# Two images loaded in six parts over three cycles; mixed weights in three slots; the centre's copy one slot later

## The chip, the cores and the metric

The kernel runs on one core of a Trainium2 chip. A core has a matrix engine (PE, with its own queue PEld for loading weights), a vector engine (DVE), a scalar engine (ACT), GpSimd (POOL), and a queue engine (SP). Each works through its own instructions in the order in which they were written, and waits for the others by semaphores alone. DMAs are issued here by SP and by POOL; all of them share sixteen DMA engines. The metric is the device time of one execution in microseconds (us), the median of several runs.

## The reference

The input is four images of 128 channels by 96 x 96 pixels, float32. Two layers follow each other, and each is a non-local block (attention of every pixel to pooled pixels of its own image):

```
g     = maxpool2(conv1x1(x, g_w, g_b))        # 64 channels, 2304 values
phi   = maxpool2(conv1x1(x, phi_w, phi_b))    # 64 channels, 2304 keys
theta = conv1x1(x, theta_w, theta_b)          # 64 channels, 9216 queries
y     = softmax(theta^T phi) g                # over the 2304 keys
out   = batchnorm(conv1x1(y, W_w, W_b)) + x
```

Per image and layer that is a 9216 x 2304 matrix of scores, its exponentials, and their product with the values. The four images are independent; the second layer of an image needs the whole of its first.

## The kernel before

**Blocks, pairs, steps, cycles.** Image and layer make a block; there are eight, in the order `ORDER`: (0,0), (1,0), (0,1), (2,0), (1,1), (3,0), (2,1), (3,1). In this text image 1 to 4 are indices 0 to 3. A block's queries go in nine *pairs* of 2 x 512, and a pair goes through the 18 key tiles in nine *steps* of two tiles, so the whole program is one loop (variable `t`) over 648 steps. Two pairs are a *cycle* of 18 steps (`CYCLE`); a step's place in its cycle is called `s`. Cycle 0 is steps 0 to 17, cycle 2 is steps 36 to 53.

**One step.** PE makes the scores of two key tiles (line 591, sixteen 64x64 matmuls), ACT takes exponentials (line 596) into one of six buffers, DVE adds them up for the denominators (line 605), and PE multiplies the exponentials of the step before by the values (line 613). Between these stands all the rest, at fixed places written out by hand. Dictionaries give the step at which something is issued: `after` (weights), `tails` (filled by `later`), `stages` (matmuls of the units, below), `loads` (images). Everything in `after` and `tails` is issued at the end of its step. No scheduler moves it.

**Ends of a pair.** Every pair's denominators are turned, inverted by DVE (`invert`, at s = 13 for the even pair, at s = 6 of the next cycle for the odd one), written by SP to a row (line 685, `stage<-both`) and spread by SP over 64 partitions in four DMAs (line 689, `halves<-stage`; here "the broadcast"). `normalise` multiplies by it at s = 1 and s = 10, and PE projects at s = 3 and s = 13 (line 705). POOL adds the result to the image in place by an accumulating DMA (line 720, `x<-halves`).

**Units: the next block's keys.** While one block is computed, the keys and values of the next are made in six *units* of 16 image rows, two per cycle in three cycles. For each, SP copies pieces of the image (lines 422 to 427: `load`, `load_rest`), POOL adds others to them by accumulating DMAs (line 419: `add_one`, `add_two`, and a last one), at s = 10, 11, 12, 12, 15 for the first unit of a cycle and at s = 0, 1, 2, 2, 4 of the next cycle for the second (`BUILDS`). PE uses the sums in four stages (`UNITS`: s = 15, 16, 0, 2 and s = 7, 8, 10, 12). The second stage (line 448) is the first that needs `add_two`. DVE then pools (line 502); for a block's first unit it also computes the keys' mean (`centring`, lines 513 and 514, one step after the fourth stage), and ACT copies that mean to the other 64 partitions (line 517). One step later `spread` writes the centred keys (ACT, lines 532 and 536). Two PSUM banks (`two_banks`) serve the units' stages, the thetas and the projections in turn.

**Weights.** `steps_mixed` makes differences and sums of the layer's g and phi weights that the units multiply by. It returns two steps: `crossed`, three ACT copies across partitions (lines 197 to 199), and `combined`, five DVE operations (lines 202 to 206) and a fourth ACT copy (line 207) that reads the result of line 204. For the first layer both stand at the end of step 9. For the second layer the list `steps` holds 13 entries (4 for g and phi, 2 mixed, 2 theta, 5 for W), three per cycle at s = 2, 7 and 11 from cycle 1 on: `crossed` at step 43, `combined` at step 47, theta at 56 and 61, W at 65, 74, 79, 83 and 92.

**Images.** Three image buffers exist. Image 1 and image 2 are loaded at the start. The others are loaded whole, six DMAs of 768 KB in a row on SP, before step 43 (image 3) and step 285 (image 4):

```
    loads = {4 * NB + 7: 2, 31 * NB + 6: 3}
...
            if t in loads:
                xs[loads[t]] = load_x(loads[t])
```

Image 4 takes the buffer of image 1, whose last store is issued at step 258. The first units that read image 3 are built from step 172 on, those of image 4 from step 334 on.

Of the kernel before, what the change touches and what calls it, by code (L numbers as in the profile page):

```python
# [9 lines left out]
F32 = mybir.dt.float32  # L10
# [7 lines left out]
B, C, CI, H, W = 4, 128, 64, 96, 96  # L18
HW = H * W
# [16 lines left out]
NB = NKT // KB  # L36
FIRST = 6
UR = 16
NU = H // UR
# [16 lines left out]
CYCLE = 2 * NB  # L56
# [6 lines left out]
def shifted_blocks(ctx: ExitStack, tc: tile.TileContext, x: bass.AP, layers, out: bass.AP, flag):  # L63
# [24 lines left out]
    nc = tc.nc  # L88
# [3 lines left out]
    xp = ctx.enter_context(tc.tile_pool(name="xp", bufs=3))  # L92
# [24 lines left out]
    for i, limit in enumerate((SUM_MAX, 1.0 / SUM_MIN)):  # L117
        nc.vector.memset(limits[:, i : i + 1], limit)

    def load_x(b, n=6):  # L120
        xt = xp.tile([C, HW], F32, tag="x", name=f"x_{b}")
        src = x[b].rearrange("c h w -> c (h w)")
        for i in range(n):
            nc.sync.dma_start(out=xt[:, ts(i, HW // n)], in_=src[:, ts(i, HW // n)])  # L124
        return xt

    def as_row(src):
# [20 lines left out]
    class Layer:  # L148
# [40 lines left out]
        def steps_mixed(self):  # L189

            low, high = slice(0, CI), slice(CI, P)
            g, phi = slice(0, CI), slice(CI, 2 * CI)
            m = self.mixed = const.tile([P, 3, CI], F32, name=f"mixed_{self.l}")
            w = self.gphi

            def crossed():
                nc.scalar.copy(m[low, 1, :], w[high, phi])
                nc.scalar.copy(m[high, 2, :], w[low, g])
                nc.scalar.copy(m[high, 1, :], w[low, phi])

            def combined():
                nc.vector.tensor_sub(m[low, 0, :], w[low, phi], m[low, 1, :])
                nc.vector.tensor_sub(m[high, 0, :], m[high, 1, :], w[high, phi])
                nc.vector.tensor_sub(m[high, 0, :], m[high, 0, :], m[high, 2, :])
                nc.vector.tensor_sub(m[high, 1, :], m[high, 2, :], m[high, 1, :])
                nc.vector.tensor_add(m[high, 2, :], w[high, g], m[high, 0, :])
                nc.scalar.copy(m[low, 2, :], m[high, 0, :])

            return [crossed, combined]

        def steps_theta(self):
            self.theta = const.tile([C, CI], F32, name=f"thetaT_{self.l}")
# [60 lines left out]
    class Block:  # L273
# [94 lines left out]
        def centring(self, n):  # L368

            centre, gphi = self.centre, self.gphi
            nc.vector.tensor_reduce(centre[CI:, :], gphi[CI:, : n * KT], AX.X, ALU.add)
            nc.vector.tensor_scalar(
                centre[CI:, :], centre[CI:, :], -1.0 / (n * KT), None, ALU.mult
            )
# [6 lines left out]
        def copied(self, keys):  # L383

            nc.scalar.copy(self.phi[:CI, keys], self.phi[CI:, keys])
# [14 lines left out]
    class Unit:  # L400
# [65 lines left out]
        def second(self):  # L466
            self.part(self.blk.w.mixed[CI:, 0, :], sums[1][CI:, :, : UN // 2], 0)
# [43 lines left out]
        def centring(self):  # L511
            centre = self.blk.centre
            nc.vector.tensor_reduce(centre[:CI, :], self.keys[:CI, 2 * UK :], AX.X, ALU.add)
            nc.vector.tensor_scalar(
                centre[:CI, :], centre[:CI, :], -1.0 / (2 * UK), None, ALU.mult
            )
            nc.scalar.copy(centre[CI:, :], centre[:CI, :])

        def parts(self):

# [6 lines left out]
        def spread(self):  # L527
            src = self.keys[:, 2 * UK :].rearrange("p (b k) -> p b k", k=32)
            planes = self.blk.planes().rearrange("p i (t k) -> p i t k", k=KT)
            for m, n, k, t in self.parts():  # L530
                dst = planes[:, :, t : t + n, ts(k, 32)]
                nc.scalar.activation(
                    dst[:, 0], src[:, m : m + n, :], AF.Identity, bias=self.blk.centre
                )
                for h in range(2):
                    nc.scalar.copy(dst[ts(1 - h, CI), 1], dst[ts(h, CI), 0])
# [233 lines left out]
    def thetas(both):  # L770
# [15 lines left out]
    ws = [Layer(l, p) for l, p in enumerate(layers)]  # L786
    ws[0].load_gphi((nc.scalar, nc.sync))
    xs = {0: load_x(0, 12)}
    ws[0].load_theta(nc.scalar)
    first_cols = columns(  # L790
# [4 lines left out]
    other_cols = columns(  # L795
        [(w, key) for w in ws for key in rest] + [(ws[1], "theta_b")], "other", nc.sync
    )
# [49 lines left out]
    for k in range(KT // 32):  # L847
        b0.square(0, k)
    xs[1] = load_x(1)


    after = {8: [other_cols], 9: ws[0].steps_mixed()}
    for i, step in enumerate(ws[0].steps_W()):
        after[10 + i] = [step]
    after[9] += [lambda: ws[1].load_gphi((nc.sync, nc.sync)), lambda: ws[1].load_theta(nc.sync)]
    after[16] = [lambda: ws[1].load_W(nc.sync)]
    steps = [lambda i=i: late_steps("gphi", i) for i in range(4)]
    steps += [lambda i=i: late_steps("mixed", i) for i in range(2)]
    steps += [lambda i=i: late_steps("theta", i) for i in range(2)]
    steps += [lambda i=i: late_steps("W", i) for i in range(5)]  # L860
    made = {}
# [1 line left out]
    def late_steps(what, i):  # L863
        if i == 0:
            made[what] = getattr(ws[1], f"steps_{what}")()
        made[what][i]()
# [8 lines left out]
    def later(t, step):  # L875
        tails.setdefault(t, []).append(step)

    for n in range(1, len(blocks)):
        cycle = (n - 1) * NP * NB // CYCLE * CYCLE
        for u in range(NU):  # L880
# [14 lines left out]
            later(when[2], unit.spread)  # L895
            for i in range(2):
                later(when[3 + i], lambda unit=unit, i=i: unit.square(i))
    loads = {4 * NB + 7: 2, 31 * NB + 6: 3}
    late = len(pairs) - 2

    ends = {
# [4 lines left out]
    for t in range(total + 1):  # L906
        q, s = 2 * (t // CYCLE), t % CYCLE
        even, odd = pairs[q : q + 2] if t < total else (None, None)
        first, second, take = None, *pending
        pending = (None, None)  # L910
        unit, stage_of = stages.get(t, (None, None))
        assert unit is None or (t not in keys and second is None)
        if t in keys:
            n, i = keys[t]
            first, *pending = blocks[n].chunks(i)
        elif unit:
            first = (unit.first, unit.second, unit.third, unit.fourth)[stage_of]
            second = unit.second_rest if stage_of == 1 else None
            take = (unit.first_sum, unit.second_sum, unit.third_sum, unit.fourth_sum)[stage_of]
        elif t < total and s == THETAS[q > 0]:  # L920
            if q < late:
                first, *pending = thetas(pairs[q + 1 : q + 3])
            else:
                first, take = odd.theta_alone()
        elif t == total - 1:
            second, take = even.multiply, even.add
        elif gone and s in PROJECT:
            pair = gone[PROJECT.index(s)]
            second, take = pair.multiply, pair.add
            later(t + STORE, pair.put)  # L930
        if t < total:
            now, j = divmod(t, NB)
            if s == 0 and q:
                gone = pairs[q - 2 : q]
            if t in loads:
                xs[loads[t]] = load_x(loads[t])
        for i in range(KB):
            if t < total:
                pairs[now].scores(j * KB + i, rowwise=stage_of == 1 and i == 1)
            if i == 0 and first:  # L940
                first()
        if second:
            second()
        for i in range(KB):
            if t < total:
                pairs[now].add_up(j * KB + i)
            if i == (stage_of == 1) and take:
                take()
        if t == 0:
            b0.batch(FIRST - 1)  # L950
        if t - 1 in keys and t < NB:
            b0.batch(keys[t - 1][1])
        if t:
            before, j = divmod(t - 1, NB)
            for k in ends.get(t, range(j * KB, (j + 1) * KB)):
                pairs[before].values(k)
        if t < total:
            for i, pair in enumerate(gone):
                if s == NORM[i]:
                    pair.normalise()  # L960
            for i, pair in enumerate((even, gone[1] if gone else None)):
                if pair is None:
                    continue
                if s in (TURNS[i], TURNS[i] + 1):
                    pair.turn(s - TURNS[i])
                sooner = q == late and i == 0
                if s == (TURNS[0] + 2 if sooner else HALVES[i]):
                    pair.add_halves()
                if s == (TURNS[0] + 2 if sooner else INVERT[i]):
                    pair.invert()  # L970
            if q == late and s == 15:
                even.normalise()
        if t == total - 1:
            odd.last_denominators()
        for i, k in squares.get(t, []):
            b0.square(i, k)
        for step in tails.pop(t, []):
            step()
        for step in after.pop(t, []):
            step()  # L980
# [323 lines left out]
```

## Time and profile before

| | |
|---|---|
| three runs | 2499.68, 2500.20, 2502.04 us (median 2500.2) |
| the profiled execution | 2500.54 us, of which its span is 2498.8 us |
| PE busy | 2474.1 us, 99% of the span |
| DVE, ACT, POOL busy | 88%, 67%, 10% |
| mean granted clock of PE | 0.997 of full |
| PE's longest wait | 13.4 us, once |

The span runs from the first to the last instruction; the remaining 1.74 us lie around it. "Busy" is the sum of an engine's instructions. A chain of waits leads back from an instruction to what released it. A line of a timeline gives start, duration, engine, kernel line, operation, written and read tiles, a count, and in brackets the idle time before and what ended it. A line of a window gives the window's length, then busy time and instructions (in brackets) of PE, PEld, DVE, ACT and POOL, the granted clock, the DMA engines' busy share, and GB/s. All start times are from the span's start.

A step is taken to begin with the first of its sixteen score matmuls in the timeline. In undisturbed cycles (all from cycle 20 on, for one) equal places take equal times to the hundredth: a cycle with two units takes 69.75 us, one without 65.23 us.

### The profile page before, as it was taken

Reading aid. Unit: us, or ns where it says so; the run is one execution under the profiler, and the core shown is the slowest. Engines: PE = TensorE matmul, PEld = TensorE weight load, DVE = VectorE, ACT = ScalarE, POOL = GpSimd, SP = SyncE. Lnnn points to the kernel's source line nnn. Section 1 sums busy time; section 2 is a strip of 40 time slices with the busy share of each in tenths; the row PEclk is TensorE's granted clock in tenths of the full one; section 3 lists DMA queues with packets and bytes.
Section 4 is the critical chain, followed back from the end, with each engine's and each line's share of the span. In section 5 each row is a group of like instructions: output and inputs, shape, how many; then the busy total and the mean of one; then the engine's idle time right before and its main releaser. Section 6 shows DMA issues by size and latency. Waiting matters only on the chain.

```text
span 2498.8 us, 56189 instructions
## 1 busy us (share of the span) xinstructions
PE 2474.1 (99%) x23391; PEld 931.2 (37%) x23391; DVE 2192.2 (88%) x2947; ACT 1671.2 (67%) x1836; POOL 254.6 (10%) x286
## 2 busy tenths in 40 slices
PE   9997999999999999999999999999999999999998
PEld 5354354333333333333333333333333333333333
DVE  7897988998889998999878998899987899877788
ACT  5665666666666676766666766676766676666665
POOL 0010111110011101110001110111100111000000
PEclk9998999999999999999999999999999999999999
DMA  6366445552366645657335673665434666333334
GB/s 185 44 83 122 52 54 70 70 71 25 26 83 95 89 52 67 93 73 132 27 27 80 99 100 35 95 80 71 53 21 45 80 81 97 43 44 43 43 36 61
DMA packets 101038, 171.72 MB, mean 69 GB/s; under 512 B 16030, under 2 KB 78120, under 8 KB 100776
## 3 DMA queue, kind: packets, MB, share of 16 engines
q1 hardware_dynamic: 65664, 94.11, 30.7%
q0 software_dynamic: 34944, 73.88, 19.5%
q8 instruction: 185, 3.03, 0.5%
q14 instruction: 77, 0.63, 0.1%
q10 hardware_dynamic: 168, 0.07, 0.0%
HBM read 19.21 MB, written 18.87 MB: 15 GB/s over the span
## 4 chain that ended last, share of the span: by engine, by line
PE 93%; DVE 3%; DMA 2%; ACT 1%; SPq 1%; issue 1%; POOL 0%; DVEq 0%; POOLq 0%; ACTq 0%
PE sc L591 42%; PE av L613 42%; PE unit_ps L442 3%; PE theta_ps L269 2%; PE W_ps L705 2%; DVE sum L605 1%; DMA halves<-stage 1%; DMA sums<-x 1%; PE unit_ps L448 1%; DMA sums<-sums 1%; PE gphi_ps L321 0%; ACT exp L596 0%; SPq L124 0%; SPq L689 0%; PE gphi_ps L269 0%
## 5 line engine op out<-in xcount | busy, mean ns | idle before, releaser
L596 ACT ACTIVATE exp<-sc,nshift 128x1024 f32<-128x1024 f32 x1296 | 1395.7, 1113 | 727.7 <-PE sc L591 703.2
L605 DVE TENSOR_TENSOR sum<-sum,exp 128x1024 f32<-128x1024 f32 x1151 | 1407.6, 1223 | 223.3 <-ACT exp L596 166.8
L591 PE MATMUL sc<-theta,phi 64*64 64x512 f32 x10368 | 1288.3, 590 | 3.0 <-ACT exp L596 2.9
L613 PE MATMUL av<-exp,gT 64*64 64x512 f32 x10368 | 1241.1, 589 | 0.0
L591 PEld LDWEIGHTS sc<-theta,phi 64*64 64x64 f32 x10368 | 415.8, 133 | 676.7 <-issue 612.9
L613 PEld LDWEIGHTS av<-exp,gT 64*64 64x64 f32 x10368 | 412.7, 133 | 684.4 <-issue 654.8
L419 POOL DMA_DIRECT2D sums<-x x84 | 81.3, 1140 | 1042.0 <-PE sc L591 543.5
L720 POOL DMA_DIRECT2D x<-halves x70 | 63.5, 907 | 1050.6 <-ACT halves L716 1028.1
L603 DVE TENSOR_TENSOR sum<-exp,exp 128x1024 f32<-128x1024 f32 x72 | 88.0, 1222 | 30.2 <-ACT exp L596 30.2
L664 DVE TENSOR_REDUCE parts<-turned 128x16 f32<-128x512 f32 x142 | 97.4, 686 | 4.9
L663 DVE STREAM_TRANSPOSE turned<-sum 128x512 f32<-128x512 f32 x142 | 100.1, 705 | 0.5
L419 POOL DMA_DIRECT2D sums<-sums x84 | 91.5, 1090 | 41.6 <-DMA sums<-sums 22.3
L620 ACT COPY halves<-av 128x1024 f32<-128x1024 f32 x71 | 72.0, 1014 | 35.4 <-PE av L613 35.4
L716 ACT ACTIVATE halves<-W_ps,shift 128x512 f32<-128x512 f32 x140 | 88.8, 693 | 0.7 <-PE W_ps L705 0.7
L502 DVE TENSOR_REDUCE stage<-stage 128x192 f32<-128x768 f32 x84 | 77.8, 941 | 0.0
L705 PE MATMUL W_ps<-halves,WT 64*64 64x512 f32 x568 | 75.2, 590 | 0.2 <-DVE stage L497 0.2
L543 DVE STREAM_TRANSPOSE gT<-stage 32x192 f32<-32x192 f32 (+1 forms) x224 | 71.5, 319 | 3.8
L269 PE MATMUL theta_ps<-x,thetaT 64*64 64x512 f32 x560 | 74.2, 589 | 0.0
L442 PE MATMUL unit_ps<-sums,mixed 64*64 64x384 f32 x504 | 69.3, 482 | 0.0
L676 DVE STREAM_TRANSPOSE four<-parts 32x32 f32<-32x32 f32 x284 | 56.4, 198 | 2.9
L699 DVE TENSOR_TENSOR halves<-halves 128x512 f32<-128x512 f32 x71 | 48.6, 685 | 7.9 <-DMA halves<-stage 7.8
L696 DVE TENSOR_TENSOR halves<-halves 128x512 f32<-128x512 f32 x71 | 48.5, 684 | 0.0
(113 smaller groups left out, 738.1 us busy)
## 6 DMA issues: line engine op xcount, KB each, us to landing
x<-halves POOLq DMA_DIRECT2D x70, 512.0 KB, 4.7
halves<-stage SPq DMA_DIRECT2D x284, 64.0 KB
out_dram<-x SPq DMA_DIRECT2D x35, 512.0 KB
sums<-x SPq DMA_DIRECT2D x42, 384.0 KB
sums<-x SPq DMA_DIRECT2D x84, 192.0 KB
sums<-x POOLq DMA_DIRECT2D x84, 192.0 KB, 4.6
sums<-sums POOLq DMA_DIRECT2D x84, 192.0 KB, 4.5
x<-in_x_dram SPq DMA_DIRECT2D x18, 768.0 KB
```

Source lines behind the costliest of these rows:

```text
L269: nc.tensor.matmul(out, lhsT=lhsT, rhs=rhs, start=step == 0, stop=step == 1)
L419: nc.gpsimd.dma_start(out=dst, in_=src, accum_op=ALU.add)
L442: nc.tensor.matmul(bank[ts(c, CI), :UN], lhsT=lhsT, rhs=rhs[:, c, :], start=True, stop=True)
L591: nc.tensor.matmul(ps[ts(c, CI), ts(h, QT)], lhsT=self.blk.keys_of(k, c, h), rhs=self.th[ts(h, CI), :], start=True, stop=True,)
L596: nc.scalar.activation(e, ps, AF.Exp, bias=nshift)
L603: nc.vector.tensor_add(self.sum, self.es[0], e)
L605: nc.vector.tensor_add(self.sum, self.sum, e)
L613: nc.tensor.matmul(self.av[ts(h, CI), ts(r, QT)], lhsT=self.blk.gT[ts(r, CI), k, :], rhs=e[ts(r, CI), ts(h, QT)], start=(k == 0), stop=(k ...
L663: nc.vector.transpose(self.turned, self.sum[:, ts(h, QT)])
L664: nc.vector.tensor_reduce(self.parts[:, ts(h, QT // SQ)], self.turned.rearrange("p (b k) -> p b k", k=SQ), AX.X, ALU.add,)
L705: nc.tensor.matmul(self.pss[h][ts(c, CI), :], lhsT=self.blk.w.W[ts(h, CI), ts(c, CI)], rhs=self.y[ts(h, CI), :], start=True, stop=True,)
L716: nc.scalar.activation(self.halves[:, ts(h, QT)], self.pss[h], AF.Identity, bias=self.blk.w.shift,)
```

## The change

Three things change.

1. Images 3 and 4 are loaded in the same six parts of 768 KB, but each part at a step of its own: image 3 at steps 43, 50, 61, 68, 79 and 86, image 4 at steps 266, 277, 284, 295, 302 and 313. All stand at s = 7 or s = 14, which is the step after one of the two `invert`s of a cycle, and so behind that one's broadcast on SP's queue.
2. `steps_mixed` returns three steps, the fourth ACT copy being the third (`copied`). For the first layer they stand at steps 7, 8 and 9. For the second layer the list grows to 14: `crossed` 43, `combined` 47, `copied` 56, theta 61 and 65, W at 74, 79, 83, 92 and 97 (so everything behind `combined` moves by one place).
3. The ACT copy of the mean (line 517) moves from `centring` to the start of `spread` of a block's first unit, one step later.

No work is added or taken away; the number of instructions on PE, DVE, ACT and POOL is the same, and so are all DMAs.

```diff
+    def new_x(b):
+        return xp.tile([C, HW], F32, tag="x", name=f"x_{b}")
+
+    def load_part(b, xt, i, n):
+        src = x[b].rearrange("c h w -> c (h w)")
+        nc.sync.dma_start(out=xt[:, ts(i, HW // n)], in_=src[:, ts(i, HW // n)])
+
     def load_x(b, n=6):
-        xt = xp.tile([C, HW], F32, tag="x", name=f"x_{b}")
-        src = x[b].rearrange("c h w -> c (h w)")
+        xt = new_x(b)
         for i in range(n):
-            nc.sync.dma_start(out=xt[:, ts(i, HW // n)], in_=src[:, ts(i, HW // n)])
+            load_part(b, xt, i, n)
         return xt
...
                 nc.vector.tensor_add(m[high, 2, :], w[high, g], m[high, 0, :])
+
+            def copied():
                 nc.scalar.copy(m[low, 2, :], m[high, 0, :])
 
-            return [crossed, combined]
+            return [crossed, combined, copied]
...
                 centre[:CI, :], centre[:CI, :], -1.0 / (2 * UK), None, ALU.mult
             )
-            nc.scalar.copy(centre[CI:, :], centre[:CI, :])
...
             planes = self.blk.planes().rearrange("p i (t k) -> p i t k", k=KT)
+            if self.u == 0:
+                nc.scalar.copy(self.blk.centre[CI:, :], self.blk.centre[:CI, :])
             for m, n, k, t in self.parts():
...
-    after = {8: [other_cols], 9: ws[0].steps_mixed()}
+    after = {8: [other_cols]}
+    for i, step in enumerate(ws[0].steps_mixed()):
+        after[7 + i] = after.get(7 + i, []) + [step]
...
-    steps += [lambda i=i: late_steps("mixed", i) for i in range(2)]
+    steps += [lambda i=i: late_steps("mixed", i) for i in range(3)]
...
-    loads = {4 * NB + 7: 2, 31 * NB + 6: 3}
+    loads = {
+        2 * CYCLE + 7 + i // 2 * CYCLE + i % 2 * 7: (2, i) for i in range(NU)
+    } | {
+        14 * CYCLE + 14 + (i + 1) // 2 * CYCLE - i % 2 * 7: (3, i) for i in range(NU)
+    }
...
             if t in loads:
-                xs[loads[t]] = load_x(loads[t])
+                b, i = loads[t]
+                if i == 0:
+                    xs[b] = new_x(b)
+                load_part(b, xs[b], i, NU)
```

## The prediction

> **What bounds the kernel now.** I read the page's busy shares first, then PE's own waits, then the chain of waits around the longest of them, then windows and timelines there.
>
> ```profile
> PE 2474.1 (99%) x23391; PEld 931.2 (37%) x23391; DVE 2192.2 (88%) x2947; ACT 1671.2 (67%) x1836; POOL 254.6 (10%) x286
> ```
>
> PE is the bound nearly everywhere: 2498.8 - 2474.1 leaves 24.7 us in the whole span. So the change can only win PE's gaps, and the next view, PE's waits, says where they lie.
>
> ```profile
> PE unit_ps L448 <- DMA sums<-sums: 13.4, 1, 13.4
> PE sc L591 <- ACT exp L596: 2.9, 5, 1.2
> PE warm_ps L818 <- POOL ident masks.py:199: 1.4, 1, 1.4
> ```
>
> One wait of 13.4 us is more than half of it. The chain of waits between 185 and 250 us shows how it came about (start, duration, what):
>
> ```profile
> 191.51 1.84 DMA stage<-both
> ...
> 197.02 2.35 SPq L124
> ...
> 204.62 15.45 DMA sums<-x
> ...
> 220.64 3.18 DMA sums<-x
> ...
> 224.69 14.03 DMA sums<-sums
> ...
> 238.86 0.58 PE unit_ps L448 x2
> ```
>
> At step 43 SP issues image 3's six loads (line 124). The unit's copy (line 422) stands behind them in the same queue and lands after 15.45 us; `add_one` therefore starts at 220.64, and `add_two` at 224.69, after the broadcast of step 49 was issued (221.94). Among that and `x<-halves` it takes 14.03 us, against a median of 4.5 for its group on the page. PE needs it in step 52.
>
> Windows over the loads, over the wait, and over whole cycles (cycles 0, 1, 2, 3, 5 and 6):
>
> ```profile
> 204.00:215.00 11.00, 10.91 (x103) 5.91 (x99) 9.65 (x17) 6.20 (x7) 0.00 (x0) 1.00 1.01 417
> 225.42:238.86 13.44, 0.01 (x1) 0.03 (x1) 3.71 (x6) 1.52 (x2) 1.39 (x2) 0.60 0.78 80
> ...
> 17.87:88.65 70.78, 69.16 (x642) 34.00 (x644) 63.62 (x105) 46.15 (x54) 4.72 (x5) 1.00 0.43 98
> 88.65:160.78 72.13, 70.99 (x676) 29.78 (x672) 66.57 (x105) 48.11 (x56) 10.90 (x12) 1.00 0.58 73
> 160.78:246.71 85.93, 72.40 (x678) 43.19 (x672) 67.74 (x100) 48.10 (x57) 10.93 (x12) 0.92 0.61 117
> 246.71:316.10 69.39, 69.39 (x661) 27.73 (x657) 64.69 (x99) 47.58 (x54) 6.38 (x7) 1.00 0.42 49
> 382.30:452.72 70.42, 70.06 (x676) 29.57 (x672) 65.22 (x99) 48.17 (x56) 10.94 (x12) 1.00 0.58 74
> 452.72:522.48 69.76, 69.76 (x678) 25.46 (x673) 65.56 (x90) 47.35 (x52) 10.90 (x12) 1.00 0.58 75
> ```
>
> Cycle 6 is what a cycle with two units costs when nothing is late. Cycle 1 is 2.4 us over it, cycle 2 16.2, cycle 5 0.7; cycle 3, whose undisturbed twin is cycle 7 at 68.78, 0.6. The granted clock (0.60 in the wait) shows a second cost: it fell to half during the wait and was full again only 3 us after it. DVE is busy 62 to 67 of 70 us in these cycles, close behind PE.
>
> The small waits, from ACT's timeline:
>
> ```profile
> 62.01 0.24 ACT L207 COPY mixed<-mixed 64x64 f32<-64x64 f32 x1 [1.49 <-DVE mixed L204]
> 107.51 0.19 ACT L517 COPY centre<-centre 64x1 f32<-64x1 f32 x1 [2.83 <-DVE centre L514]
> 210.63 0.24 ACT L207 COPY mixed<-mixed 64x64 f32<-64x64 f32 x1 [3.11 <-DVE mixed L204]
> 400.85 0.19 ACT L517 COPY centre<-centre 64x1 f32<-64x1 f32 x1 [2.51 <-DVE centre L514]
> ```
>
> Each holds the exponentials queued behind it, and PE's scores wait for those.
>
> **The change, part by part.** Step lengths are from the timeline, each against the same place in undisturbed cycles.
>
> *Image 3's loads.* Step 52 took 19.21 us, not 3.76: 15.45, of which 13.44 is the wait and most of the rest the half clock. A part is 786,432 bytes; at the window's 417 GB/s it holds the DMA engines 1.9 us. SP issues one in 0.4 to 2.4 us, between waits for DVE (at line 685) of up to 34; POOL's order does not change. In its new place the first part (step 43) stands behind the broadcast issued at 193.49 to 196.97 and ahead of line 422, which waits for PE's third stage until about 201.8. What does `add_two` then do? In cycle 1, same layout without loads, the broadcast's last packets end at 133.6 and `add_two`'s at 147.0, 13.4 later. In cycle 2 the broadcast ends at 204.5; plus 1.9, plus 13.4, `add_two` ends at 219.8. PE needs it at 224.4 (line 448's place in step 52 without the late steps before it), and the next broadcast is issued at about 221. Margins 4.6 and 1.2 us, all in the clock of before (earlier gains move everything alike): no wait. What is left is the lateness cycle 1 has at the same place (`spread` waits for DVE's pooling, steps 33 and 34 together 0.98 over); with DVE a little less late here I take 0.3. Gain 15.1. Were the margin gone, the cost is the first rival's.
>
> The part of step 50 lands behind its broadcast by about 235, the next line 422 is due at about 233, and its sums are needed 28 us later: free. The part of step 79 goes ahead of line 422 at 350.48; that unit's `add_two` ended at 369.0, is needed at 376.2 and meets a broadcast at 373.0: 1.9 us fit. Those of steps 61 and 68 have no sums behind them for 14 steps; that of 86 stands as that of 50 does.
>
> *Image 4's loads.* Nothing to win: all six at 1131.96 cost PE nothing. The parts of steps 266 and 284 precede a build at s = 0 as that of step 50 does (and before, all six stood there at 285). The part of step 277 goes ahead of line 422 at 1107.88; `add_two` ended at 1122.5, is needed at 1130.6, meets a broadcast at 1128.45: 1.9 us fit. The last three have no build behind them until step 334. The buffer's last store, of step 258, is eight steps old at step 266, so SP does not wait on it. Zero. Bounds for all new places together: 0 and, at the worst, the rival.
>
> *Mixed, second layer.* The copy waited 3.11 us in step 47; steps 48 and 49 were 0.52 and 0.20 long. At step 56 its operand is nine steps old; 0.24 us of ACT fit its 1.3 us pauses per step. DVE won 1.05 us of idle there, so it is not late in turn. Gain 0.72.
>
> *Mixed, first layer.* Step 10 took 5.43 for 3.43, step 11 3.63 for 3.43: 2.2. The crossed copies (0.72) move to step 7, where ACT pauses over 1 us; `combined` (1.1) lies on DVE a step earlier. But DVE idled only 1.05 in this wait and has no further pause before step 15; there PEld already waits 0.38 us in step 16 for DVE's line 464. So PE, 2.2 sooner, waits about 1.1 for DVE at step 16. Gain 1.05; bounds 0.5 (DVE later still) and 2.2.
>
> *The centre's copy.* In the first of these blocks steps 22 and 23 were 0.98 over; DVE idled 0.54 there and is then full until step 35, with steps 31, 33 and 34 already late. Gain 0.55, bounds 0.4 and 1.0. In cycle 5 0.67 over; DVE's `make_shift` (0.9 us) also leaves step 92 for step 97, where it may cost 0.2 at step 105: gain 0.5. In cycle 19 0.1. In the other four blocks ACT waited as well and PE lost nothing. `spread`, which waits for the same DVE results a step later, pays 0.19 us of ACT, under its pauses.
>
> *Theta and W one place later.* Cycle 3 was 0.6 over because DVE was 2.4 to 2.7 late around step 65; 0.84 us of transposes leave step 56, and 0.84 replaces 0.58 at step 65. Gain 0.5, bounds 0 and 0.6. The second layer's W is first used at step 183: no wait.
>
> Sum: 15.1 + 0.72 + 1.05 + 0.55 + 0.5 + 0.1 + 0.5 = 18.5 us. Span 2498.8 - 18.5 = 2480.3; the profiled execution 2500.54 - 18.5 = 2482.0. The median of the runs stood 0.34 below that execution, so I forecast 2481.7.
>
> [...]
>
> **The rivals.**
> 1. *The sums still run into a broadcast (the slower side).* If a part holds the queue longer than the margin, `add_two` starts under the broadcast and takes 14 us again: in cycle 2 it would end near 235, 10.6 after it is needed, with the half clock 12. One place alone leaves 2494, still faster. From two on (24) it is slower, 2505.7; with steps 88 and 286 too 2517.7. That takes a part of 5.9 us at step 79 (4.0 from 369.0 to 373.0, and the 1.9) against 1.9: unlikely, 3% for slower, 5% for one place or a partial stall.
> 2. *The loads were not the cause.* Broadcast and `x<-halves` collide anyway, step 52 stays: only 3.4 won, 2496.8. Against it: cycles 1, 5 and 6 have the same broadcasts without the wait. 2%.
> 3. *DVE takes back all small gains.* PE's waits on ACT only hide DVE's lateness: 15.1 alone, 2485.1. 10%.
> 4. *Nothing is taken back.* 15.45 + 0.72 + 2.2 + 0.98 + 0.67 + 0.1 + 0.6 = 20.7: 2479.5. 7%.
>
> My forecast has the remaining 73%.
>
> **How the numbers follow.** The range goes from rival 4 less the runs' spread (0.9) to rival 3 plus a partial stall of 2 us: 2478.6 to 2487. What a measurement can tell from no change is 0.2%, 5 us; all cases but rival 1's slow end, and the 3.4 us of rival 2, are beyond it on the fast side: faster 0.94, same 0.03, slower 0.03.
>
> **What would show it.** PE's waits lose the line for 448; cycle 2 is near 70 us and its clock 1.00; the half clock appears at the ends only. ACT's wait before lines 207 and 517 vanishes, while step 16's PEld wait grows to over 1 us. Image 4's cycles stay at 69.75. Wrong, if line 448 or 442 waits for `sums<-sums` or `sums<-x` in steps 52, 88 or 286, or DVE's wait before line 699 grows to several us.

## The result, and the profile after

The changed kernel takes 2483.45 us (median of 6 runs, 2482.49 to 2483.91). Beside it, the kernel before took 2501.06 (median of 6, 2499.68 to 2502.40): 17.6 us less, a ratio of 0.9929 with a 95% interval of 0.9916 to 0.9942. The forecast was 2481.7, with a range of 2478.6 to 2487.0.

Lines of kernel.py are numbered differently from here on: 456 was 448, 450 was 442, 430 was 422, 427 was 419, 125 was 124, 698 was 689, 600 was 591, 472 was 464, 215 was 207. First the busy shares of the page, then PE's own waits (waiting instruction, releaser, us in total, times, longest).

```profile
span 2482.1 us, 56196 instructions
...
PE 2472.2 (100%) x23391; PEld 1602.5 (65%) x23391; DVE 2192.5 (88%) x2947; ACT 1667.2 (67%) x1836; POOL 254.2 (10%) x286
```

```profile
PE warm_ps L827 <- POOL ident masks.py:199: 1.4, 1, 1.4
PE sc L600 <- ACT exp L605: 0.9, 3, 0.4
PE W_ps L714 <- DVE stage L505: 0.4, 2, 0.2
```

The line of 13.4 us is gone, and nothing of its kind has come; the waits for exponentials fell from 2.9 to 0.9, and the small one below them, PE waiting for DVE, grew from 0.2 to 0.4. PE is nearly as busy as before (2472.2 us for 2474.1): most of the time came out of its gaps, which fell from 24.7 to 9.9 us in all. PEld's busy time grew from 931.2 to 1602.5 with the same loads, each as long as before (133 ns); a run below shows where that comes from.

Cycles 0, 1, 2, 3 and 5 (window; its length, then busy time of PE, PEld, DVE, ACT, POOL; granted clock, DMA share, GB/s):

```profile
17.80:87.28 69.48, 69.04 (x642) 37.02 (x644) 63.38 (x105) 46.03 (x54) 4.71 (x5) 1.00 0.43 100
87.28:159.03 71.75, 71.27 (x678) 41.85 (x674) 66.73 (x105) 48.27 (x57) 10.90 (x12) 1.00 0.59 74
159.03:229.32 70.29, 70.05 (x678) 45.80 (x672) 66.77 (x100) 47.77 (x56) 10.89 (x12) 1.00 0.63 86
229.32:299.13 69.81, 69.64 (x662) 42.20 (x656) 65.46 (x96) 47.73 (x56) 6.36 (x7) 1.00 0.49 72
365.34:435.19 69.85, 69.85 (x677) 40.66 (x673) 65.03 (x98) 48.63 (x57) 10.91 (x12) 1.00 0.66 87
```

Cycle 2 fell from 85.93 to 70.29, its clock is 1.00 throughout. Cycle 0 won 1.3, cycles 1 and 5 about half a microsecond each. Cycle 3 *grew*, from 69.39 to 69.81.

How the sums and the broadcast stand now, from the timelines of SP and of POOL in cycle 2:

```profile
195.25 2.35 SPq L125 DMA_DIRECT2D x<-in_x_dram  x1
200.22 0.67 SPq L430 DMA_DIRECT2D sums<-x  x1
...
219.96 3.45 SPq L698 DMA_DIRECT2D halves<-stage  x4
```

```profile
212.69 1.20 POOL L427 DMA_DIRECT2D sums<-sums  x1
214.74 0.89 POOL L729 DMA_DIRECT2D x<-halves  x1 [0.84 <-ACT halves L725]
```

One load stands ahead of the unit's copy; `add_two` is issued at 212.69, 7.3 us ahead of the broadcast at 219.96. Before, it was issued 2.8 us behind it.

### The profile page after: what moved, and what is told of

The parts are those of the page before. It is cut to its first block, busy times and chain, and to the rows that moved or that the text cites. A ratio compares the mean times of both kernels' runs of the same rounds, so it can differ in the third digit from the quotient of the medians.

```text
span 2482.1 us, 56196 instructions
## 1 busy us (share of the span) xinstructions
PE 2472.2 (100%) x23391; PEld 1602.5 (65%) x23391; DVE 2192.5 (88%) x2947; ACT 1667.2 (67%) x1836; POOL 254.2 (10%) x286
## 3 DMA queue, kind: packets, MB, share of 16 engines
HBM read 19.21 MB, written 18.87 MB: 15 GB/s over the span
## 4 chain that ended last, share of the span: by engine, by line
PE 94%; DVE 4%; DMA 1%; issue 1%; ACT 0%; SPq 0%; DVEq 0%; POOL 0%; POOLq 0%; ACTq 0%
PE av L622 42%; PE sc L600 42%; PE unit_ps L450 3%; PE theta_ps L277 2%; PE W_ps L714 2%; DVE sum L614 2%; DMA halves<-stage 1%; PE unit_ps L456 0%; PE gphi_ps L329 0%; ACT exp L605 0%; PE gphi_ps L277 0%; DVE four L685 0%; DVE turned L672 0%; DVE stage L510 0%; DVE parts L673 0%
## 5 line engine op out<-in xcount | busy, mean ns | idle before, releaser
L600 PE MATMUL sc<-theta,phi 64*64 64x512 f32 x10368 | 1459.7, 589 | 0.9 <-ACT exp L605 0.9
L622 PE MATMUL av<-exp,gT 64*64 64x512 f32 x10368 | 1386.2, 589 | 0.0
L622 PEld LDWEIGHTS av<-exp,gT 64*64 64x64 f32 x10368 | 717.5, 133 | 379.4 <-issue 49.8
L600 PEld LDWEIGHTS sc<-theta,phi 64*64 64x64 f32 x10368 | 716.2, 133 | 371.2 <-issue 41.8
L714 PE MATMUL W_ps<-halves,WT 64*64 64x512 f32 x568 | 90.8, 590 | 0.4 <-DVE stage L505 0.4
L277 PE MATMUL theta_ps<-x,thetaT 64*64 64x512 f32 x560 | 89.9, 589 | 0.0
L450 PE MATMUL unit_ps<-sums,mixed 64*64 64x384 f32 x504 | 78.9, 482 | 0.0
L685 DVE STREAM_TRANSPOSE four<-parts 32x32 f32<-32x32 f32 x284 | 56.4, 198 | 2.9
L708 DVE TENSOR_TENSOR halves<-halves 128x512 f32<-128x512 f32 x71 | 48.8, 687 | 8.9 <-DMA halves<-stage 8.8
L714 PEld LDWEIGHTS W_ps<-halves,WT 64*64 64x64 f32 x568 | 39.7, 133 | 23.0 <-DVE stage L505 2.2
```

The costliest lines, as they stand in the source:

```text
L277: nc.tensor.matmul(out, lhsT=lhsT, rhs=rhs, start=step == 0, stop=step == 1)
L450: nc.tensor.matmul(bank[ts(c, CI), :UN], lhsT=lhsT, rhs=rhs[:, c, :], start=True, stop=True)
L600: nc.tensor.matmul(ps[ts(c, CI), ts(h, QT)], lhsT=self.blk.keys_of(k, c, h), rhs=self.th[ts(h, CI), :], start=True, stop=True,)
L622: nc.tensor.matmul(self.av[ts(h, CI), ts(r, QT)], lhsT=self.blk.gT[ts(r, CI), k, :], rhs=e[ts(r, CI), ts(h, QT)], start=(k == 0), stop=(k ...
L714: nc.tensor.matmul(self.pss[h][ts(c, CI), :], lhsT=self.blk.w.W[ts(h, CI), ts(c, CI)], rhs=self.y[ts(h, CI), :], start=True, stop=True,)
```

## Experiments

The theory (A): PE lost its time in step 52 because `add_two`, put off by loads that stood ahead of the unit's copy in SP's queue, met the broadcast; the small parts add to that independently, but where DVE is full it takes part of them back. Rivals are named with each run; steps and waits are from one profiled execution of each kernel, times from all its runs. A step's length is the distance between two steps' first score matmuls in the timeline.

**Loads alone, and all but the loads.** The first run puts the new loads (and `new_x`, `load_part`) into the kernel before. The second puts the old loads into the changed kernel:

```diff
-    loads = {
-        2 * CYCLE + 7 + i // 2 * CYCLE + i % 2 * 7: (2, i) for i in range(NU)
-    } | {
-        14 * CYCLE + 14 + (i + 1) // 2 * CYCLE - i % 2 * 7: (3, i) for i in range(NU)
-    }
+    loads = {4 * NB + 7: 2, 31 * NB + 6: 3}
...
-                b, i = loads[t]
-                if i == 0:
-                    xs[b] = new_x(b)
-                load_part(b, xs[b], i, NU)
+                xs[loads[t]] = load_x(loads[t])
```

> Kernel before with the loads of images 3 and 4 spread as in the change, nothing else. Theory A (the six loads in a row caused the wait in step 52, and the small parts of the change add up on their own): step 52 falls from 19.21 to about 4.3 us, cycle 2 from 85.93 to about 71; steps 10, 22, 48 and 94 keep their lateness (5.43, 4.36, 4.60, 4.05); the median lies 14.5 to 15.2 us under the kernel before, near 2486. Theory B (loads were not the cause, rival 2 of the prediction): step 52 stays near 19, the time within 1 us of before.

> The changed kernel with both images loaded whole again before steps 43 and 285. Theory A (small parts are independent of the loads): the small terms alone, about 1.4 in cycle 0, 0.4 in cycle 1, 0.7 in cycle 2, 0.6 in cycle 5 won and 0.4 in cycle 3 lost: 2.5 to 3 us under the kernel before, near 2498; step 52 waits near 13 us again. Theory C (the vector engine takes back all small gains, rival 3): within 1 us of before.

Measured: loads alone 2486.21 us (2485.79 to 2487.24; ratio 0.9942, interval 0.9925 to 0.9959), all but the loads 2498.44 (2496.55 to 2499.97; ratio 0.9988, interval 0.9979 to 0.9998), beside 2501.25 for the kernel before. So 15.0 and 2.8 us; together 17.8, where the whole change won 17.6. The two halves add up within the scatter of the second one's runs, which is 3.4 us. In step 52 they are not quite independent: it was 4.61 us with the loads alone and 4.28 with both, and 20.37 with all but the loads, where the kernel before had 19.21. PE's waits of the second run have the old line again:

```profile
PE unit_ps L456 <- DMA sums<-sums: 13.9, 1, 13.9
```

Rival 2 (the loads were not the cause) falls, and so does rival 3 (DVE takes back all small gains): 2.8 us are left, though this interval just reaches 0.9998. Firmer is the other comparison: the changed kernel's median is 2.8 us under that of the loads alone, and the two ranges do not overlap.

In cycle 3 the two runs tell more. Step 67 was 4.52 before, 4.76 with the loads alone, 4.69 with all but the loads, 4.95 with both. So its growth of 0.43 has two nearly independent parts, 0.24 and 0.17.

**Is it the spread, or what stands behind the loads?** All six parts of image 3 in a row again, but before step 61, after which no sums are built for 21 steps:

```diff
-    loads = {
-        2 * CYCLE + 7 + i // 2 * CYCLE + i % 2 * 7: (2, i) for i in range(NU)
-    } | {
-        14 * CYCLE + 14 + (i + 1) // 2 * CYCLE - i % 2 * 7: (3, i) for i in range(NU)
+    loads = {61: [(2, i) for i in range(NU)]} | {
+        14 * CYCLE + 14 + (i + 1) // 2 * CYCLE - i % 2 * 7: [(3, i)] for i in range(NU)
     }
...
-            if t in loads:
-                b, i = loads[t]
+            for b, i in loads.get(t, []):
```

> The changed kernel with image 3's six parts in a row before step 61, where the next sums are built 21 steps later. Theory A (what counts is that no sums stand behind the loads in the queue, not that the parts are spread): same as the changed kernel within 1 us, near 2483.4; no wait of line 456; step 52 at 4.3 and cycle 3 near 69.8. Theory D (the spread over three cycles is needed, since six parts in a row hold the queue for 11 us and some broadcast, or the accumulating copies, come late): cycle 3 grows by several us, the time to 2486 or more.

Measured: 2483.47 us (2482.78 to 2484.26; ratio 0.9929, interval 0.9913 to 0.9946), the changed kernel's time. SP's timeline and the windows of cycles 2 and 3:

```profile
265.99 7.08 SPq L125 DMA_DIRECT2D x<-in_x_dram  x6
```

```profile
159.54:229.84 70.30, 70.06 (x678) 45.90 (x673) 66.77 (x100) 47.76 (x56) 10.89 (x12) 1.00 0.59 74
229.84:299.64 69.80, 69.63 (x661) 42.33 (x656) 65.44 (x96) 47.73 (x56) 6.36 (x7) 1.00 0.60 117
```

Both as in the changed kernel (70.29, 69.81), with the six loads in the second one (117 GB/s for 72 in the changed kernel, with two). The spread is not needed; a place with nothing urgent behind it in the queue is. Theory D falls.

**How many parts fit ahead of the sums?** Four parts before step 43 and two before step 61; in the other run three and three (the new lines alone; the rest of the edit is that of the run above):

```diff
+    loads = {43: [(2, i) for i in range(4)], 61: [(2, i) for i in range(4, NU)]} | {
...
+    loads = {43: [(2, i) for i in range(3)], 61: [(2, i) for i in range(3, NU)]} | {
```

> The changed kernel with four of image 3's parts before step 43 and two before step 61. Each further part ahead of line 430 should put off the second accumulating copy (add_two) by 1.9 us. With one part add_two was issued at 212.69 and its packets ended near 217, the broadcast of step 49 was issued at 219.96. Theory A (the cost comes only when add_two meets the broadcast): three parts more put its issue to about 218.4 and its end to 222.6, into the broadcast, where it slows down: a wait of line 456 in step 52 of 1 to 8 us. If a part costs much more than 1.9 us in the queue: as before, over 10 us. If the broadcast does not matter: under 1 us.

> The changed kernel with three of image 3's parts before step 43 and three before step 61. Theory A (1.9 us per part, harm only once the second accumulating copy meets the broadcast): its issue moves from 212.69 to about 216.5, its end to 220.7, at the very start of the broadcast's packets (221): wait of line 456 in step 52 under 1 us, step 52 between 4.2 and 5.3. Theory B (every part ahead costs PE its own time, about 1.9 to 3.8 us): step 52 at 8 us or more.

Measured, one execution each: with three parts step 52 was 4.28, the changed kernel's length (2483.76 us); with four it was 8.22 (2486.84 us). PE's waits, and POOL's and SP's timelines, with four parts:

```profile
PE unit_ps L456 <- DMA sums<-sums: 2.5, 1, 2.5
```

```profile
218.11 1.20 POOL L427 DMA_DIRECT2D sums<-sums  x1
218.64 1.59 POOL L729 DMA_DIRECT2D x<-halves  x1
```

```profile
219.58 12.27 SPq L698 DMA_DIRECT2D halves<-stage  x4
```

POOL's and SP's timelines with three parts:

```profile
215.62 1.20 POOL L427 DMA_DIRECT2D sums<-sums  x1
216.15 1.59 POOL L729 DMA_DIRECT2D x<-halves  x1
```

```profile
217.39 0.70 SPq L694 DMA_DIRECT2D stage<-both  x1
222.88 3.52 SPq L698 DMA_DIRECT2D halves<-stage  x4
```

With four parts `add_two` was issued at 218.11 (expected 218.4; three parts 215.62, expected 216.5), the broadcast 1.5 us later, its issue alone taking 12.27 us instead of 3.45. `add_two` then took 6.9 us to land. With three parts the broadcast was issued only at 222.88, when `add_two` had landed (220.22, 4.6 us after its issue), so the two did not meet. `x<-halves` stood 0.5 us behind `add_two` in both runs, so it alone is not what slows `add_two`. What put the broadcast off with three parts was the row that it spreads and has to wait for: the packets of the row's write (line 694) ran from 219.8 to 222.2, among those of `x<-halves` (218.9 to 222.4). With four parts the row was written by 219.0, before the first packet of `x<-halves` (221.3).

Counted from the start of cycle 2, `add_two` was issued after 52.3 us with no part ahead (the run before: 211.82), 53.7 with one, 56.4 with three and 59.4 with four: 1.4 to 3.0 us per part, and that is free until the meeting. Then step 52 is 3.9 us longer at four parts and 14.9 at six. Theory B (each part costs PE its own time) falls, and its 3.8 us per part no run shows.

**The copy of the mean back in `centring`.**

```diff
             )
+            nc.scalar.copy(centre[CI:, :], centre[:CI, :])
...
-            if self.u == 0:
-                nc.scalar.copy(self.blk.centre[CI:, :], self.blk.centre[:CI, :])
```

> The changed kernel with the mean's copy where it was, in centring. Steps 22 and 23 should be 0.9 to 1.0 us longer again, steps 94 and 95 0.3 to 0.7 (the shift's five operations no longer stand in step 92). Theory A (the vector engine takes back part of the gain later in cycle 1): steps 26 and 31 become shorter by about 0.6 in return, so the whole is only 0.4 to 1.2 us slower than the changed kernel. Theory E (no taking back): 1.3 to 1.7 us slower.

Measured: 2484.85 us (2484.38 to 2485.16; ratio to before 0.9935, interval 0.9920 to 0.9950), 1.4 above the changed kernel's 2483.45 of an earlier set. Cycle 1: step 22 was 1.18 longer, step 23 0.05, and steps 26 and 31 0.26 and 0.34 shorter: of 1.23 us DVE gives 0.60 back, as theory A had it. But the total is over A's 1.2. The expectation missed two things. In cycle 5 steps 94 and 95 grew by 0.05 only and step 106 by 0.56 instead; why there, no run here shows. And steps 184 and 346 grew by 0.20 each, where the same wait had cost nothing and 0.05 in the kernel before. The traces show why it costs there now: the four streams in which PE runs its matmuls (see the next run) begin step 184 within 0.015 us of each other in the kernel before, and the first exponentials end 3.31 us after the step's start. Here the last stream begins 0.28 us behind the first, the exponentials end at 3.57, and a step at this place lasts 3.43 in itself.

**Theta and W at their old steps**, with only the mixed weights' copy left at step 56:

```diff
+    late_copied = steps.pop(6)
     for i, step in enumerate(steps):
         after[CYCLE + i // 3 * CYCLE + (2, 7, 11)[i % 3]] = [step]
+    after[3 * CYCLE + 2].append(late_copied)
```

> The changed kernel with the second layer's theta and W weights at the steps that they had before (56, 61, 65, 74, 79, 83, 92); only the copy of the mixed weights stays at step 56. Theory A (cycle 3 became slower because 0.84 us of transposes stand at step 65 in place of 0.45 us of scaling, while the relief at step 56 is lost in the vector engine's waits for the exponentials in steps 57 to 59): step 67 falls from 4.95 to about 4.5, cycle 3 from 69.81 to about 69.4; step 94 may be up to 0.2 longer, since the shift's operations return to step 92; 0.2 to 0.5 us faster than the changed kernel. Theory F (cycle 3's loss comes from the loads of steps 61 and 68): cycle 3 stays at 69.8.

Measured: 2482.93 us (2482.68 to 2483.47; ratio to before 0.9928, interval 0.9913 to 0.9943), 0.5 below the changed kernel, which is within the runs' spread. Step 67 fell from 4.95 to 4.77, not to 4.5, and cycle 3 to 69.65. So the shift is worth 0.18 of cycle 3's loss; the rest, 0.24, is what the loads alone showed. The loads themselves are not it: with six of them in cycle 3 instead of two, step 67 was 4.95 as well. It comes with the vanished wait. In the kernel before, step 60's first exponentials ended 2.24 us after the step began; in the changed kernel, with the loads alone and in this run it was 2.49, and DVE's additions began equally late after the exponentials (1.60 us in step 61 in the kernel before and with the loads alone). With four parts, where PE waited 2.51 us, it was 2.26, and step 67 was 4.72; with three parts, and no wait, 4.96. The weight loads around the start of step 60 show what differs, in the kernel before, the changed one and the run with four parts:

```profile
270.32 0.16 PEld L591 LDWEIGHTS sc<-theta,phi 64*64 64x64 f32 x4 [0.27 <-issue]
```

```profile
252.50 1.70 PEld L600 LDWEIGHTS sc<-theta,phi 64*64 64x64 f32 x16
```

```profile
256.75 0.18 PEld L600 LDWEIGHTS sc<-theta,phi 64*64 64x64 f32 x4 [0.25 <-issue]
```

PE runs these 64x64 matmuls four at a time, in four streams: each takes 0.59 us, and the next four begin 0.43 after the first four. In the kernel before, step 60's four streams begin within 0.025 us of each other; in the changed kernel two of them begin 0.27 us after the other two. The step is as long (4.29), but its last scores, and so its exponentials, come 0.25 us later. Behind cycle 0, all eleven changes of this offset by over 0.03 us in the kernel before, and eight of the nine in the changed one, come at a step in which PE was held up (0.09 us or more over the undisturbed length; at the ninth it was 0.02). At step 44 it was 0.27 in the kernel before too, and the wait in step 52 brought the streams together. The offset is also why PEld is busy longer in the changed kernel: the loads of four streams that run apart overlap less (four took 0.16 us and left 0.27 free in the kernel before; in the changed one sixteen took 1.70 without a pause).

**The weights' work in DVE's pauses.** What cycles 0 to 3 still have over their undisturbed length should be DVE's lateness. So the first layer's shift goes from step 14 to 18, and the second layer's fourteen steps go to places where DVE has pauses and the next use is still ahead:

```diff
-    for i, step in enumerate(ws[0].steps_W()):
-        after[10 + i] = [step]
+    for i, step in zip((10, 11, 12, 13, 18), ws[0].steps_W()):
+        after[i] = [step]
...
-    for i, step in enumerate(steps):
-        after[CYCLE + i // 3 * CYCLE + (2, 7, 11)[i % 3]] = [step]
+    slots = (72, 73, 75, 76, 77, 81, 82, 88, 90, 144, 145, 147, 148, 151)
+    for t, step in zip(slots, steps):
+        after[t] = [step]
```

> The changed kernel with the weights' work taken out of the cycles in which the vector engine is full: the first layer's shift from step 14 to 18, the second layer's fourteen steps to 72, 73, 75, 76, 77, 81, 82, 88, 90, 144, 145, 147, 148 and 151, where it has pauses. Theory A (what is left over the undisturbed length in cycles 0 to 3 is the vector engine's lateness from this work): step 16 falls from 4.44 to 3.8, cycle 1 from 71.75 to 69.8, cycle 2 from 70.29 to 69.8, cycle 3 from 69.81 to 68.8, cycle 5 to 69.75, and no other cycle grows by over 0.3: 3.5 to 4.3 us under the changed kernel, near 2479.3. Rival: the lateness comes from the units and from queue effects, not from the weights: under 1 us.

Measured: 2478.99 us (2478.56 to 2479.89; ratio to before 0.9912, interval 0.9898 to 0.9925), 4.5 below the changed kernel, a little more than expected. By step lengths cycles 0 to 5 give 4.0 and the last two steps 0.35. Cycles 1 to 3:

```profile
86.58:156.33 69.75, 69.75 (x676) 39.01 (x672) 65.42 (x100) 48.33 (x56) 10.87 (x12) 1.00 0.60 76
156.33:226.09 69.76, 69.76 (x677) 39.01 (x673) 65.38 (x89) 47.36 (x52) 10.89 (x12) 1.00 0.63 87
226.09:294.87 68.78, 68.78 (x660) 38.01 (x656) 64.20 (x90) 47.48 (x54) 6.37 (x7) 1.00 0.49 73
```

Cycles 1, 2 and 3 have their undisturbed lengths (69.75, 69.75, 68.78) to 0.01 us, and PE has no gap in them. Cycle 0 keeps 0.28 in step 16 (4.04, expected 3.8). This version beats both kernels.

## Why the prediction was right, by its own steps

| step of the prediction | predicted gain, us | measured, from step lengths |
|---|---|---|
| image 3's loads (step 52) | 15.1 | 14.93 |
| mixed, second layer (steps 48, 49) | 0.72 | 0.71 |
| mixed, first layer (steps 10, 11; taken back in 16) | 1.05 | 1.98 - 0.67 = 1.31 |
| the mean's copy, cycle 1 (22, 23; taken back in 26, 31) | 0.55 | 0.97 - 0.60 = 0.37 |
| the mean's copy and the shift, cycle 5 (94, 95; 106) | 0.5 | 0.67 - 0.09 = 0.58 |
| cycle 19 | 0.1 | 0.10 |
| theta and W one place later (cycle 3) | 0.5 | -0.43 |
| image 4's loads | 0 | 0 (cycles 14 to 16 within 0.03) |
| sum | 18.5 | 17.6 |

The span shrank by 16.7, not 17.6, mainly for two things at its end: step 646 took 0.17 longer, and the stretch from the last step's start to the end 0.82 (19.89 for 19.07 us), of which 0.67 lies behind the last store's issue. That stretch took 19.0 to 19.9 us in the ten traces. The medians, over several runs, are 17.6 apart. That the sum of the other terms came out nearly as predicted is partly luck: the first layer's mixed weights won 0.26 more and cycle 5 0.08 more, the loads 0.17 less and the mean's copy 0.18 less.

*Right in mechanism and size: the loads.* The prediction had `add_two` end 59.0 us after the start of cycle 2 (219.8 less 160.78); it landed after 58.2 (217.26 less 159.03). Its margins were 4.6 us until PE needs the sums and 1.2 until the broadcast, at 1.9 us per part. The four-part and three-part runs bear out the order of events: it is the broadcast that decides. The 1.2 was too small: three parts, two more than the change has, still fitted, since the broadcast itself was put off to 222.88. Two parts more moved `add_two` by 2.7 us and three more by 5.7, each from the start of its cycle 2: 1.4 and 1.9 us a part, so the window's 1.9 stood.

*Right: DVE takes back a part.* In cycle 0 PE came 2 us earlier to step 16 and found DVE unfinished, as predicted there. The weight loads (PEld) of that step:

```profile
82.06 0.14 PEld L456 LDWEIGHTS unit_ps<-stage,mixed 64*64 64x64 f32 x2 [0.95 <-DVE stage L472]
```

The wait was 0.38 before; I had expected over 1. And ACT no longer waits before the copy of the mixed weights: its timeline shows no idle time before line 215 at 59.80.

*Wrong: cycle 3.* The step that failed reads "0.84 us of transposes leave step 56, and 0.84 replaces 0.58 at step 65. Gain 0.5". Two errors. First, DVE can only be relieved of lateness that it has. After step 56 it was 0.3 to 0.6 us late, at steps 57 to 59, and with the transposes gone it reached zero and waited for exponentials; by step 62 the relief that was left was 0.27 us (2.41 to 2.14), and the work added at step 65 used it up and more: 0.17 to 0.18 lost. Second, DVE's lateness was taken from a trace in which PE had just come out of its long wait, with its four streams together and exponentials 0.25 us sooner. Without the wait step 67 is 0.24 to 0.26 longer, with the weights at their old steps (4.52 to 4.76) and at the new ones (4.69 to 4.95); in the last run, where DVE had been relieved and the offset of the streams was 0.10, it took 4.29.

The median forecast was 1.75 us low. 0.93 of that is cycle 3's term, and 0.86 the base: the three runs shown had a median of 2500.2, the six beside the changed kernel 2501.06.

## What to carry to other kernels

A long transfer cost nothing by itself here; ask what stands behind it in its queue, and what the late ones will then collide with. Here six loads in a row were free at step 61 and cost 15 us at step 43. Where a second engine is nearly as full as the bound, count a won wait only up to that engine's idle time in it, and count a relief only up to the lateness that the engine has at that moment; then move work to where the engine idles, not merely later.

## What had not been expected of the hardware

In the run with four parts (one execution) PE waited 2.51 us, and the granted clock stayed full during it and for 1.4 us after; only then it fell to half, for 3.4 us, with PE at work. Windows over the wait, the 1.4 us after it, the half-clock stretch and the time behind:

```profile
222.58:225.09 2.51, 0.00 (x1) 0.03 (x1) 2.42 (x5) 1.28 (x2) 0.00 (x0) 1.00 0.98 125
225.09:226.46 1.37, 1.37 (x20) 1.06 (x24) 1.06 (x1) 0.00 (x0) 0.82 (x1) 1.00 0.86 118
226.46:229.87 3.41, 3.41 (x23) 1.33 (x19) 2.15 (x5) 1.11 (x1) 0.00 (x0) 0.50 0.76 85
229.87:235.00 5.13, 5.13 (x52) 2.19 (x48) 2.90 (x4) 2.83 (x3) 0.00 (x0) 1.00 0.55 25
```

So a wait of 2.5 us cost 3.9 in step 52 and 0.2 in step 53. In the kernel before the half clock lasted 13.65 us, from 228.23 to 241.88, four times as long; there too it began 2.8 us after the wait did (225.42). What the run with four parts adds is that 2.51 us of idleness were enough there, and that the price in clock was paid only after work had resumed. What sets the start and the length of the half clock, these two stretches do not show.
